# A three-layer graph attention kernel: partial sums stored in the last quarter of a round, loads reordered behind them, two copies moved to ScalarE, one PSUM bank exchanged

## The chip, the cores and the metric

The kernel runs on one core of one Trainium2 chip. The metric is the device time of one execution in microseconds: the median of the runs of one kernel. Differences are judged between kernels run on the same chip.

## The reference

There are 6250 nodes with 64 features each and 206250 directed edges (each of 100000 drawn pairs in both directions, and one loop per node), sorted by destination. Each edge has 64 features of its own, the same in all three layers. A layer is a transformer convolution:

```
q, k, v = x@Wq+bq, x@Wk+bk, x@Wv+bv          # per node
e       = edge_attr @ We                      # per edge
alpha   = sum(q[dst] * (k[src] + e)) / 8      # per edge
w       = softmax of alpha over the edges of one destination
x       = relu(segment_sum((v[src] + e) * w, dst) + x@Ws + bs)
x       = layer_norm(x) * gamma + beta        # after layers 0 and 1 only
```

After the third layer a log-softmax over the features is taken, the input is added, and a last layer norm without scale gives the output.

## The kernel before

**Tiling.** Edges are cut into tiles of 128, six tiles make a chunk (768 edges), four chunks make a unit (`LB = 4`, `TC = 6`). There are 67 whole units and a last one of four tiles. Since edges are sorted by destination, all destinations of a chunk lie within 32 nodes (`W = 32`), so the four chunks of a unit are stacked on 4 x 32 partitions. The weights are folded into the node side, so that an edge's score is a dot product of a 128-vector of its destination (`q`) with the source's 64 features and the edge's own 64 features.

**What is kept in DRAM.** `eaS` holds edge features transposed (feature by edge), `eaP` holds them with edges on partitions, `maskS` a mask that removes the wrong destinations, `keyS` the keys of which the picks (below) are made, `qq` the destination vectors, and `part0` and `part1` one partial sum of 32 rows by 130 columns for each chunk (weighted features, the running maximum, the weight total). The chunks alternate between `part0` and `part1`.

**Two sources of a node's features.** Some of a unit's tiles are gathered by GpSimd, one indirect DMA for each tile (`gather`, L601). The others are *picked*: TensorE multiplies one-hot matrices `hot` (made on VectorE from `keys`, L1335) with the nodes' features that lie in SBUF as `parts` (L1387), and VectorE copies the right block out of PSUM (L1356, L1359). A round picks 12 or 14 of 24 tiles in layers 1 and 2.

**Layer 0 also sorts.** While the first layer runs, `sorter` moves the edges of each unit so that the picked tiles have their sources in known ranges of nodes. A `Move` has four parts of three steps. `row` makes one-hot rows `hit` (L1074), `products` multiplies raw edge features with them (L1085) and, for the destination codes, the `stamp` (L1094). `impress` (L1059) fills `stamp` from `misc` with two VectorE copies (L1064 and L1065) in a move's fourth part for the next move. `index` (L1157) decodes the result: it takes two PSUM tiles from bank "a", `pi` (matmuls L1167) and `pk` (matmuls L1165); VectorE reads `pi` (L1175, L1184), ScalarE reads `pk` (L1186). `Move.across` (L1123) transposes the moved edge features through bank "a" (L1128) and writes `eaP`, `drain` writes `eaS`, `Move.shade` writes `maskS`. Bank "a" has two buffers, bank "g" one.

**A round.** The order of instructions on each engine is the order in which the program writes them; nothing is reordered later, and the SP queue, which issues nearly all loads and stores, works off its list in that order, too. In round `u` of a layer (the loop at L1904) the pieces are these:

- start: the weighted sums of unit `u-2` (`Unit.sums`, L1746, into bank "g", copied by ScalarE to `part`, L1753), and the first half of the scores of unit `u-1` (`Unit.scores`, L1692, which reads `featT` of all four chunks)
- in quarter `j` (0 to 3) of the round: transposes of chunk `j` of unit `u` (`turn`, L1679, copied to `featT` by ScalarE, L1682), a gate that lets GpSimd gather a later chunk (L633), and a quarter of the picks of unit `u+1`
- `turn(j)` begins with `more`, which asks for the edge features of chunk `j+1` of the same unit (`featT <- eaS`, L1659). So `featT` of chunks 1, 2 and 3 is asked for in quarters 0, 1 and 2
- quarter 0 also asks for `eaP` of unit `u+2` (`refill`, L570), runs one step of whatever layer ending is due (`close_up`: `finish` loads the partial sums of up to 512 nodes, L1486, and makes their new features), asks for the four `q` of unit `u+1` (L1633) and, by `Unit.across`, for `featT` of chunk 0 of unit `u+1`
- quarter 1 stores the four partial sums of unit `u-2` (`Line.store`, `Unit.store`, L1757) and appends the `finish` of those nodes that are complete; its first step is taken by the next `close_up`, in quarter 0 of the next round
- quarter 2 asks for the mask of unit `u+1` (`Unit.shade`, L1607) and the keys of unit `u+2` (`decode`, L1831)

`featT` has six buffers. A unit is "placed" when it has gone through the sorter: all whole units in layers 1 and 2, and from unit 3 on in layer 0. Only in layer 0 does SP also load `raw` edge features for the sorter (L1033, eight loads in a move, asked for four parts ahead).

Of the kernel before, what the change touches and what calls it, by code (L numbers as in the profile page):

```python
# [29 lines left out]
BITS = 5  # L30
FAR = 2.0**100
GS = 4
LB = 4
TC = 6
# [395 lines left out]
def main_path(  # L430
# [53 lines left out]
    nc = tc.nc  # L484
# [44 lines left out]
    def ps(tag):  # L529
        return psum.tile([P, 512], F32, tag=tag, name=f"ps_{tag}", bufs={"a": 2, "x": 2}.get(tag, 1))  # L530
# [7 lines left out]
    def placed(layer, k):  # L538

        return k < NT and (layer > 0 or k >= U0)  # L540

    def picked(layer, k):

        if not placed(layer, k) or k < LEAD[layer]:
            return 0
        return 2 if layer == 0 and k <= len(groups) // 2 else PICKS[layer][k % len(PICKS[layer])]
# [501 lines left out]
    class Move:  # L1048
# [10 lines left out]
        def impress(self):  # L1059

            misc, self.pos = marks[self.c0 // GC]
            self.at = (self.c0 % GC) * TC
            spots = slice(self.at, self.at + LB * TC)
            nc.vector.tensor_copy(self.stamp[:, :, :BITS], misc[:, :BITS, spots].rearrange("p r c -> p c r"))  # L1064
            nc.vector.tensor_copy(  # L1065
                self.stamp[:, :, ROW_P : ROW_K + 1], misc[:, BITS:, spots].rearrange("p r c -> p c r")
            )

# [88 lines left out]
        def index(self):  # L1157

            k = self.k
            n = NP  # L1160
            pi = ps("a")[:, : TC * 3 * LB].rearrange("p (t v c) -> p t v c", t=TC, v=3)
            pk = ps("a")[:LB, : n * P].rearrange("c (t h e) -> c t h e", t=n, h=2)
            those = self.to[:, : n * P].rearrange("p (t h e) -> p t h e", t=n, h=2)
            for h in range(2):
                nc.tensor.matmul(pk[:, :, h], keyc[:, h], those[:, :, h], start=True, stop=True)  # L1165
            for t in range(TC):
                nc.tensor.matmul(  # L1167
                    pi[:, t].rearrange("p v c -> p (v c)"),
                    self.to[:, t * P : (t + 1) * P],
                    pickc.rearrange("p v c -> p (v c)"),  # L1170
                    start=True,
                    stop=True,
                )
            mine = src_b[:, k * LB * TC : (k + 1) * LB * TC]
            nc.vector.tensor_tensor(  # L1175
                mine.rearrange("p (c j t) -> p t c j", j=2, t=TC),
                pi[:, :, 0].rearrange("p t (c j) -> p t c j", j=2),
                shift.unsqueeze(2).to_broadcast([P, TC, LB // 2, 2]),
                ALU.add,
            )  # L1180
            nc.vector.tensor_scalar(mine, mine, N - 1, None, ALU.min)
            for h in range(2):
                there = slice(h * P // 2, (h + 1) * P // 2)
                nc.vector.tensor_copy(kbs[there, k], pi[there, :n, 1 + h])  # L1184
            key = small.tile([LB, n, P], FP16, name="key", bufs=1)
            nc.scalar.copy(key.rearrange("c t e -> c (t e)"), pk.rearrange("c t h e -> c (t h e)"))  # L1186
            nc.scalar.dma_start(keyS[k].rearrange("t c e -> c t e"), key)
            moved.add(k)
# [400 lines left out]
    class Unit:  # L1589
# [31 lines left out]
        def ask(self):  # L1621

            self.b = []
            for j in range(self.m):
                b = nc.values_load(
                    base[0:1, self.c + j : self.c + j + 1],
                    engines=(ENG.SP,),
                    min_val=0,
                    max_val=NB * P,
                    skip_runtime_bounds_check_because="the least of a chunk's nodes, NB*128 at most",  # L1630
                )
                self.b.append(b)
                nc.sync.dma_start(self.q[:, j * W : (j + 1) * W], qq[:, ds(b, W)])  # L1633
# [152 lines left out]
    chunks = {}  # L1786
# [30 lines left out]
    def move(n):  # L1817

        for _ in range(n):
            next(sorting, None)  # L1820
            serve()
# [3 lines left out]
    def decode(layer, k):  # L1825

        n = picked(layer, k) if k < NT else 0
        if n and (layer, k) not in keys and (layer or k in moved):
            room = max(PICKS[layer]) * P
            keys[layer, k] = stock[0].tile([P, room], FP16, name="keys")  # L1830
            nc.sync.dma_start(  # L1831
                keys[layer, k][:, : n * P],
                keyS[k].rearrange("t c e -> (t c e)")[: n * P].partition_broadcast(P),
            )
# [43 lines left out]
    def step(n=1):  # L1878
        for _ in range(n):
            advance()  # L1880
# [3 lines left out]
    def close_up(n=1):  # L1884
        step(n)
        for _ in range(n):
            advance(ending)
        if lacking or held:
            reload(current[0] + 1)
# [5 lines left out]
    for layer in range(L):  # L1895
        line = Line(layer)
        assert not picked(layer, 0)

        def free(u, j):
            lead = 2 * LB if not layer else min(2 * LB, LB + u)  # L1900
            release(layer, u * LB + j + (0 if not layer else 1) + lead, nc.scalar.copy)

        picker = Picker(layer)
        for u in range(NU - 2):  # L1904
            this = chunks[layer, u]
            picking = picker.batch(u + 1)
            n = picked(layer, u + 1)
            n //= 2
            pace = 0 if layer else 6 if u < 3 else 3
            while not opened:  # L1910
                move(1)
            line.sums(u - 2)
            line.products(u - 1, 0)
            if waiting:
                active.append(waiting.pop(0))
            for j in range(LB):
                picker.quarter = j
                if j == 2:
                    line.weights(u - 1, 0)
                this.turn(j)  # L1920
                if j == 0:
                    line.refill(u - 2)
                free(u, j)
                if j == 0 and layer:
                    line.most(u - 1, 0)
                    line.products(u - 1, 1, "m")
                if j == 1:
                    line.store()
                    if not layer and placed(0, u + 1):
                        line.most(u - 1, 1)  # L1930
                a, b = -(-n * j // LB), -(-n * (j + 1) // LB)
                if layer:
                    for i in range(max(b - a, 1)):
                        next(picking, None)
                        if not i and not j:
                            line.most(u - 1, 1)
                if j == 0:
                    close_up()
                else:
                    step()  # L1940
                if not layer:
                    move(pace - pace // 2)
                    if j == 0:
                        line.most(u - 1, 0)
                    for _ in range(b - a):
                        next(picking, None)
                    move(pace // 2)
                    picker.evacuate()
                if j == 0:
                    if not layer:  # L1950
                        line.products(u - 1, 1)
                        if not placed(0, u + 1):
                            line.most(u - 1, 1)
                    ask(layer, u + 1)
                    chunks[layer, u + 1].across()
                if j == 2:
                    line.weights(u - 1, 1)
                    chunks[layer, u + 1].shade()
                    decode(layer, u + 2)
            assert next(picking, None) is None  # L1960
            if any(not pair for _, pair, *_ in picker.swaps):
                picker.flush()
            picker.ready.update(keys)
            picker.aim()
            for k in range(u + 2, u + 4):
                decode(layer, k)
# [14 lines left out]
        u = NU - 2  # L1981
# [74 lines left out]
def kernel(tc: tile.TileContext, *args):  # L2056
    nc = tc.nc
    with tc.tile_pool(name="flag", bufs=1) as pool:
        irregular = pool.tile([1, 1], I32, name="irregular")
        with tc.manual_schedule(engines={ENG.PE, ENG.DVE, ENG.Activation, ENG.SP, ENG.Pool}):  # L2060
            main_path(tc, *args, irregular)
        flag = nc.values_load(irregular[0:1, 0:1], min_val=0, max_val=1, skip_runtime_bounds_check_because="a comparison")
        with tc.If(flag > 0):
            general_path(tc, *args)
# [34 lines left out]
```

## Time and profile before

| | |
|---|---|
| runs of the kernel before | 4369.96, 4365.49 and 4349.52 us, median 4365.49 us |
| the profiled execution | 4357.57 us, of which the span is 4355.8 us |
| mean granted TensorE clock | 0.926 |
| DMA | 728.90 MB, mean 167 GB/s |
| the nodes' features of layers 1 and 2 are split into `parts` (L1269) | from 1958.6 us, the last at 3175.9 us |

The span divides into layer 0 with the sorter (up to about 2.0 ms), layer 1 (to about 3.15 ms) and layer 2. In the tables of the profile a row of instructions has its line, engine, operation, what it writes and reads, its count, the busy time and the mean of one in ns, and the idle time of its engine just before it with what ended that idle time. A row of waits has the waiting engine and line, the releaser, the microseconds in total, how many times, and the longest one; "issue" stands for a wait that the profile can put down to nothing. SPq is the list of SP. A window's row has its stretch, then busy us and counts of PE, PEld (weight loads), DVE (VectorE), ACT (ScalarE) and POOL (GpSimd), the granted TensorE clock, the DMA share and GB/s.

### The profile page before, as it was taken

Reading aid. Unit: us, or ns where it says so; the run is one execution under the profiler, and the core shown is the slowest. Engines: PE = TensorE matmul, PEld = TensorE weight load, DVE = VectorE, ACT = ScalarE, POOL = GpSimd, SP = SyncE. Lnnn points to the kernel's source line nnn. Section 1 sums busy time; section 2 is a strip of 40 time slices with the busy share of each in tenths; the row PEclk is TensorE's granted clock in tenths of the full one; section 3 lists DMA queues with packets and bytes.
Section 4 is the critical chain, followed back from the end, with each engine's and each line's share of the span. In section 5 each row is a group of like instructions: output and inputs, shape, how many; then the busy total and the mean of one; then the engine's idle time right before and its main releaser. Section 6 shows DMA issues by size and latency. Waiting matters only on the chain.

```text
span 4355.8 us, 108102 instructions
## 1 busy us (share of the span) xinstructions
PE 3555.1 (82%) x34711; PEld 2476.2 (57%) x34711; DVE 3376.9 (78%) x11892; ACT 2305.6 (53%) x5860; POOL 2706.5 (62%) x2642
## 2 busy tenths in 40 slices
PE   4788888888889898985888888788768878777886
PEld 2345555555555555554666666666556666666664
DVE  6678888888888888865787778787667777777775
ACT  1345555555555555553555555555545556555555
POOL 5467665656666665654776666666367666666662
PEclk9889999999999999997999999999879999999997
DMA  5656666656666666665776667766657666666663
GB/s 124 170 167 189 173 179 166 177 155 181 177 165 185 168 173 158 180 174 136 178 188 167 169 172 180 180 167 172 160 133 182 172 170 172 174 161 169 173 171 88
DMA packets 783500, 728.90 MB, mean 167 GB/s; under 512 B 485192, under 2 KB 610050, under 8 KB 782928
## 3 DMA queue, kind: packets, MB, share of 16 engines
q1 hardware_dynamic: 630436, 508.46, 45.5%
q0 software_dynamic: 84224, 86.41, 10.4%
q10 hardware_dynamic: 68268, 127.03, 8.2%
q8 instruction: 283, 4.64, 0.5%
q14 instruction: 289, 2.37, 0.2%
HBM read 562.78 MB, written 158.68 MB: 166 GB/s over the span
## 4 chain that ended last, share of the span: by engine, by line


## 5 line engine op out<-in xcount | busy, mean ns | idle before, releaser
L601 POOL DMA_INDIRECT feat<-x,gate x1460 | 1451.2, 994 | 706.4 <-issue 315.6
L601 POOL DMA_INDIRECT feat<-in_x,gate x1100 | 1181.8, 1074 | 724.0 <-ACT gate L633 421.0
L1387 PE MATMUL ps_x<-parts,hot 128*128 128x256 f32 x6864 | 1033.1, 299 | 173.5 <-DVE feat L1359 157.3
L1387 PEld LDWEIGHTS ps_x<-parts,hot 128*128 128x128 f32 x6864 | 905.8, 199 | 326.7 <-issue 231.2
L1682 ACT COPY featT<-ps_a 64x384 f32<-64x384 f32 x1588 | 753.7, 475 | 538.0 <-PE ps_a L1679 521.9
L1359 DVE COPY_PREDICATED feat<-which,ps_x 128x128 f32<-128x128 int32 x2574 | 779.0, 303 | 88.7
L1335 DVE TENSOR_SCALAR hot<-keys,rank 128x512 fp32r<-128x512 f16 (+1 forms) x1172 | 471.5, 470 | 59.8 <-DMA keys<-keyS 59.2
L1356 DVE COPY feat<-ps_x 128x128 f32<-128x128 f32 x858 | 246.2, 287 | 301.4 <-PE ps_x L1387 295.6
L1679 PE MATMUL ps_a<-ident,feat 128*128 128x128 f32 x2380 | 433.9, 291 | 53.5 <-DMA feat<-x,src_b 31.2
L1692 PE MATMUL ps_s<-featT,q 128*32 128x384 f32 x2134 | 306.3, 505 | 191.2 <-issue 104.6
L1074 DVE TENSOR_SCALAR hit<-ruler,pos 128x384 bf16<-128x384 f16 x1608 | 457.4, 325 | 5.9 <-PE ps_m L1094 5.9
L1679 PEld LDWEIGHTS ps_a<-ident,feat 128*128 128x128 f32 x2380 | 285.1, 147 | 251.6 <-issue 190.2
L1720 ACT ACTIVATE prob<-prob,part 128x768 f32<-128x768 f32 x204 | 190.3, 933 | 251.1 <-DVE part L1719 155.8
L1746 PE MATMUL ps_g<-feat,probT 128*32 128x128 f32 x9672 | 315.3, 276 | 2.0 <-ACT probT L1737 2.0
L1085 PE MATMUL ps_x<-hit,raw 128*64 128x384 bf16 x1608 | 298.7, 367 | 0.1
L1085 PE MATMUL ps_x<-hit,rest 128*64 128x384 bf16 x1608 | 281.1, 346 | 0.0
L1085 PE MATMUL ps_x<-hit,end 128*64 128x384 bf16 x1608 | 280.5, 345 | 0.0
L1746 PEld LDWEIGHTS ps_g<-feat,probT 128*32 128x32 f32 x9672 | 262.9, 111 | 27.8 <-ACT probT L1737 5.7
L1737 ACT COPY probT<-ps_p 128x384 f32<-128x384 f32 x399 | 191.8, 481 | 124.7 <-PE ps_p L1734 78.9
L1734 PE MATMUL ps_p<-ident,prob 128*128 128x128 f32 x1197 | 212.3, 288 | 37.1 <-ACT prob L1720 33.8
L1692 PEld LDWEIGHTS ps_s<-featT,q 128*32 128x32 f32 x2134 | 71.2, 111 | 267.2 <-issue 194.2
L1706 DVE CUSTOM_DVE_ANT_0 prob<-ps_s,shade 128x384 f32<-128x384 f32 x204 | 112.9, 553 | 129.6 <-PE ps_s L1692 120.3
(266 smaller groups left out, 5288.5 us busy)
## 6 DMA issues: line engine op xcount, KB each, us to landing
featT<-eaS SPq DMA_DIRECT2D x792, 192.0 KB
feat<-eaP SPq DMA_DIRECT2D x134, 768.0 KB
raw<-in_ea SPq DMA_DIRECT2D x536, 96.0 KB
eaS<-eT ACTq DMA_DIRECT2D x134, 384.0 KB
eaP<-feat ACTq DMA_DIRECT2D x128, 384.0 KB
shade<-maskS SPq DMA_DIRECT2D x198, 192.0 KB
keys<-keyS SPq DMA_DIRECT2D x66, 448.0 KB
keys<-keyS SPq DMA_DIRECT2D x66, 384.0 KB
```

Source lines behind the costliest of these rows:

```text
L601: nc.gpsimd.indirect_dma_start(out=feat[:, c, t, 0], out_offset=None, in_=xts[layer][:, :], in_offset=bass.IndirectOffsetOnAxis(ap=index[: ...
L1074: nc.vector.tensor_scalar(hit, ruler, self.pos[:, at : at + 1], None, ALU.is_equal)
L1085: nc.tensor.matmul(self.px[j * D : (j + 1) * D, :HE], self.parts[2 * h + i].thirds[part][:, j, t * D : (t + 1) * D], self.hits[h, 2 * i + ...
L1335: nc.vector.tensor_scalar(hot[:, h], keys[self.layer, k][:, first : first + n], rank[:, h : h + 1], None, ALU.is_equal)
L1356: nc.vector.tensor_copy(found, px[:, :, 0])
L1359: nc.vector.copy_predicated(found, which[:, first : first + 2, b].bitcast(I32).unsqueeze(2).to_broadcast([P, 2, D]), px[:, :, b],)
L1387: nc.tensor.matmul(px[:, v].rearrange("p b d -> p (b d)"), hot[:, h, (2 * pair + v) * P : (2 * pair + v + 1) * P], those[:, i, b0 + h * KB ...
L1679: nc.tensor.transpose(pt[:, t * P : (t + 1) * P], rows[:, 2 * t * D : 2 * (t + 1) * D], ident)
L1682: nc.scalar.copy(featT[:, :, h, :], pt[h * D : (h + 1) * D, : n * P].rearrange("d (i e) -> d i e", e=P))
L1692: nc.tensor.matmul(p_s[rows, :w], self.q[:, rows], self.featT[j][:, cols], start=True, stop=True)
L1734: nc.tensor.transpose(p_t[:, t, :n], self.prob[:n, at : at + P], ident[:n, :n])
L1746: nc.tensor.matmul(p_g[rows, :].rearrange("n (h d) -> n h d", h=2), self.probT[:, t, rows], batch[:, j, t], start=(t == 0), stop=(t == sel ...
```

## The change

Five edits, all in the order or the place of existing work; nothing that is computed changes.

1. The two copies that fill `stamp` run on ScalarE instead of VectorE.
2. `pi` in `index` takes bank "g" instead of bank "a".
3. `line.store()` moves from quarter 1 (after `turn(1)`) to the end of quarter 3.
4. For placed units `chunks[layer, u + 1].across()`, the load of `featT` of the next unit's chunk 0, moves from quarter 0 to quarter 2.
5. In quarter 2 the keys are asked for first, then that `featT`, then the mask; before, it was the mask, then the keys.

```diff
-            nc.vector.tensor_copy(self.stamp[:, :, :BITS], misc[:, :BITS, spots].rearrange("p r c -> p c r"))
-            nc.vector.tensor_copy(
+            nc.scalar.copy(self.stamp[:, :, :BITS], misc[:, :BITS, spots].rearrange("p r c -> p c r"))
+            nc.scalar.copy(
                 self.stamp[:, :, ROW_P : ROW_K + 1], misc[:, BITS:, spots].rearrange("p r c -> p c r")
             )
...
-            pi = ps("a")[:, : TC * 3 * LB].rearrange("p (t v c) -> p t v c", t=TC, v=3)
+            pi = ps("g")[:, : TC * 3 * LB].rearrange("p (t v c) -> p t v c", t=TC, v=3)
...
                 if j == 1:
-                    line.store()
                     if not layer and placed(0, u + 1):
                         line.most(u - 1, 1)
...
                     ask(layer, u + 1)
-                    chunks[layer, u + 1].across()
+                    if not placed(layer, u + 1):
+                        chunks[layer, u + 1].across()
                 if j == 2:
                     line.weights(u - 1, 1)
-                    chunks[layer, u + 1].shade()
                     decode(layer, u + 2)
+                    if placed(layer, u + 1):
+                        chunks[layer, u + 1].across()
+                        chunks[layer, u + 1].shade()
+                if j == 3:
+                    line.store()
```

## The prediction

> **What bounds the kernel now.** I read first the page's table of engines, then busy time by stage, then the waits of TensorE, then the SP queue beside TensorE over two rounds, since the change is mostly to SP's list.
>
> ```profile
> PE 3555.1 (82%) x34711; PEld 2476.2 (57%) x34711; DVE 3376.9 (78%) x11892; ACT 2305.6 (53%) x5860; POOL 2706.5 (62%) x2642
> ```
>
> ```profile
> 300.00:1850.00 1550.00, 1380.77 (x13799) 834.64 (x13795) 1339.57 (x4747) 853.73 (x2175) 983.65 (x914) 0.95 0.66 174
> 2100.00:3050.00 950.00, 786.54 (x7858) 621.17 (x7859) 734.83 (x2536) 523.81 (x1367) 635.51 (x638) 0.95 0.69 175
> 3300.00:4250.00 950.00, 763.87 (x7655) 602.25 (x7654) 730.44 (x2554) 541.31 (x1378) 626.35 (x629) 0.95 0.68 172
> ```
>
> The first stretch lies in layer 0, the others in layers 1 and 2. In layer 0 PE is busy for 89% (1380.77 of 1550) and DVE for 86%: the two take turns waiting for each other. In layers 1 and 2 PE has 82% and DVE 77%, so nobody is full and a wait must be looked for.
>
> ```profile
> PE ps_s L1692 <- issue: 104.6, 41, 4.6
> PE ps_s L1692 <- DMA featT<-eaS: 63.6, 31, 3.9
> ```
>
> ```profile
> DVE prob L1706 <- PE ps_s L1692: 49.6, 19, 5.4
> ```
>
> ```profile
> DVE prob L1706 <- PE ps_s L1692: 56.9, 20, 6.2
> ```
>
> The first two rows are of the whole run, the DVE rows of the windows 2100:3050 and 3300:4250. PE stands before the scores for 168.2 us in 72 waits, 2.3 us each; neither row is among the waits of 300:1850, so this is a thing of layers 1 and 2. The list of SP, then PE, around one such wait:
>
> ```profile
> 2765.92 4.97 SPq L1757 DMA_DIRECT2D part<-part  x4
> 2771.00 0.45 SPq L1659 DMA_DIRECT2D featT<-eaS  x1
> ...
> 2772.64 0.45 SPq L1659 DMA_DIRECT2D featT<-eaS  x1
> 2773.40 0.32 SPq L570 DMA_DIRECT2D feat<-eaP  x1
> 2774.23 2.80 SPq L1633 DMA_DIRECT2D q<-qq  x4
> 2778.24 1.10 SPq L1659 DMA_DIRECT2D featT<-eaS  x2
> 2779.61 6.36 SPq L1757 DMA_DIRECT2D part<-part  x4
> 2786.07 0.47 SPq L1659 DMA_DIRECT2D featT<-eaS  x1
> ```
>
> ```profile
> 2768.11 1.52 PE L1746 MATMUL ps_g<-feat,probT 128*32 128x128 f32 x48
> 2769.45 0.82 PE L1692 MATMUL ps_s<-featT,q 128*32 128x384 f32 x6
> 2774.59 1.32 PE L1692 MATMUL ps_s<-featT,q 128*32 128x384 f32 x2 [4.32 <-issue]
> ...
> 2791.47 1.52 PE L1746 MATMUL ps_g<-feat,probT 128*32 128x128 f32 x48
> ```
>
> A round starts at 2768.11 with the sums. Six of eight score matmuls run (chunks 0 to 2), the two of chunk 3 wait 4.32 us. Their `featT` was issued only at 2771.00, behind four stores that held SP for 4.97 us; from issue to use are 3.6 us. So the "issue" row is the same wait as the featT row: the last edge features of a unit are asked for too late, because the stores stand ahead of them. Why the stores are slow, and how full SP is:
>
> ```profile
> SPq L1757 <- DMA part<-part: 397.8, 208, 4.8
> SPq L1659 <- PE ps_s L1692: 325.5, 49, 14.0
> SPq L570 <- PE ps_g L1746: 188.8, 68, 9.4
> SPq L1757 <- DMA feat<-eaP: 123.6, 61, 3.8
> SPq L1633 <- DMA qq<-qs: 65.8, 16, 8.7
> ```
>
> ```profile
> SPq L570 <- PE ps_g L1746: 85.4, 30, 7.3
> ```
>
> ```profile
> L1607 SPq DMA_DIRECT2D shade<-maskS x57: 356/522/1400, 2108.0 to 3042.5; - x57
> ```
>
> The last two are of 2100:3050. A store waits until the one two places before it, into the same table, has landed (1.9 us a time). With one mask a round, 950 us hold 57 rounds of 16.7 us, of which SP waits for PE (L570) only 1.5: SP is occupied, its DMA waits included, for 15.2 us.
>
> **The change part by part: layers 1 and 2.** With the stores at the end and chunk 0 of the next unit later, chunk 3's `featT` follows `eaP`, four `q` and chunk 2. In the round above it would take the place of the second `featT` of the pair at 2778.24, about 5.4 us after `eaP`, instead of 12.7 (2786.07 - 2773.40): 7 us sooner, against waits of at most 4.6. What moves back has room: chunk 0, mask and stores of this round are read first in the next round's end or later, since unit `u+1` is scored at the start of round `u+2`. The stores stand ahead of the next round's `eaP` and `q`, of units that are summed and scored rounds later. A `finish` loads the table right behind the stores, in quarter 0 as before, and may wait up to 4.8 us for a landing; its data is used a round later, so I cost it at nothing, and at 16 late `q` (8.7 us at most, the qq row) the 7 us still cover the wait that is left.
>
> What is late next? While PE stands, DVE first makes `hot` and then idles: 106.5 us in the two windows of 57 rounds each (49.6 + 56.9), so 123 us for the 132 rounds of two layers. Where both stand the time is surely lost; the other 45 us of 168.2 may only turn into PE waiting for DVE. I take 120 us. Bounds: 168 if all comes back; below, nothing, if SP is simply too full (a rival).
>
> **Layer 0: keys.**
>
> ```profile
> DVE hot L1335 <- DMA keys<-keyS: 59.2, 28, 4.2
> ```
>
> In 28 rounds DVE stands 2.1 us for keys. They now go ahead of the mask, of chunk 0 and of the stores, some 5 us of SP's list (4.97 for the stores alone), but also behind `raw` loads that wait for PE's progress; an advance of 2.1 us on average is enough. Gain up to 59.2 us of DVE; I take it all, the waits being at most 4.2.
>
> **Stamps.**
>
> ```profile
> L1065 DVE COPY stamp<-misc 128x72 bf16<-128x72 bf16 x67 | 20.6, 308 | 0.0
> L1064 DVE COPY stamp<-misc 128x120 bf16<-128x120 bf16 x67 | 18.0, 268 | 0.0
> ```
>
> ```profile
> 1003.89 0.26 DVE L1064 COPY stamp<-misc 128x120 bf16<-128x120 bf16 x1
> ...
> 1004.17 0.55 DVE L1074 TENSOR_SCALAR hit<-ruler,pos 128x384 bf16<-128x384 f16 x2
> ```
>
> By their busy time DVE gets rid of 38.6 us, but they overlap their neighbours: from the first's start to the next instruction's are 0.28 us, times 67 makes 19. I take 20, the row in place. ScalarE takes them up:
>
> ```profile
> L992 ACT CAST misc<-spare x17: 246/266/273, 66.8 to 1818.7; 128x96 bf16<-128x96 int32 x16, 128x72 bf16<-128x72 int32 x1
> ```
>
> ```profile
> ACT to L1115 <- PE ps_m L1094: 181.3, 130, 5.3
> ```
>
> A like copy of 96 columns takes 266 ns there, so two take about 0.53 us, 36 us in all. They stand in the queue ahead of the copies that wait for PE's stamp matmuls (1.4 us a time), which covers them; without that cover PE would wait for ScalarE 0.53 us in 67 moves, the 36 us. The stamp's own reader is a part later. The Trainium skill, "ScalarE: Activation LUTs", section "Rules for kernel authors", speaks against this edit: simple operations belong on VectorE, which it has up to about 3 times faster in bf16. The DVE rows above show no such speed on these strided copies; by the rule the pair would be 1.7 us on ScalarE, 0.3 over the cover, and the sum 23 us worse, an estimate from that page.
>
> **The bank of `pi`.**
>
> ```profile
> PE ps_a L1167 <- ACT key L1186: 19.5, 14, 3.9
> PE ps_a L1128 <- DVE kbs L1184: 18.2, 11, 3.4
> PE ps_a L1167 <- ACT featT L1682: 14.8, 17, 2.3
> PE ps_a L1167 <- DVE xT L1434: 8.0, 4, 2.2
> ```
>
> In 300:1850 PE waits 60.5 us because `pi` needs one of two buffers of bank "a", or holds one. In "g" it follows the sums of the same round, copied out long before, and in some rounds a layer ending's product. Worth 0 to 60 us of PE.
>
> DVE's side is then 59 + 20 = 79 us, PE's 60. Since each spends much of its idle time waiting for the other, the sum of both can't be had; I take their mean, 70 us. Bounds: 30 (half the smaller) to 139 (both). SP's 325.5 us (L1659) stay: with six buffers, chunk 2's `featT` now meets the wait that chunk 0's met, for the same matmuls.
>
> **Sum.** 120 + 70 = 190 us off the profiled 4357.57 gives 4168; that execution lies 8 us under the median of the runs, 4365.49, and against this the forecast is 4175 us. Its own range, from the bounds with 60 to 168 for layers 1 and 2, is 4060 to 4275.
>
> **The rivals.**
>
> *Another wait takes over in layers 1 and 2.* PE's stall is also when DVE makes `hot` for the next picks:
>
> ```profile
> 2769.56 3.05 DVE L1335 TENSOR_SCALAR hot<-keys,rank 128x512 fp32r<-128x512 f16 x8
> ```
>
> That is 3.05 us of work beside 4.32 of stall, 71%. If this share of the 120 us comes back as PE waiting for DVE's `hot` and block copies, 35 are left, and with layer 0's 70 it is 4260 us. For it: PE and DVE are both near 80%. Against it: sums, scores and transposes follow on PE in the same time and cover `hot`.
>
> *The keys come no sooner*, because SP in layer 0 is held at chunk 2 (the 325.5 row) and at `raw`: the change doesn't do there what it says. Layer 0 then gives (20 + 60) / 2 = 40: 4205 us.
>
> *More than the stalls*: without them the clock rises too.
>
> ```profile
> 2180.00:2289.00 109.00, 92.36 (x979) 74.25 (x978) 92.38 (x319) 66.15 (x172) 83.73 (x83) 1.00 0.73 186
> ```
>
> Here the granted clock is 1.00 against 0.95 in the windows. If layers 1 and 2 got there, PE would save 0.05 x 1900 = 95 us; half of it, as DVE must follow, makes 4125 us. Against it: layer 0 has 0.95 without these stalls. The Trainium skill, "TensorE: Matmul & The Clock Gate", section "Part 1: The HAM clock gate", has the clock halved only after about 3.4 us of idleness; by that rule most stalls, 2.3 us on average, cost no clock, and the sum stays at 4175.
>
> *Slower: SP becomes the bound.* SP has 15.2 of 16.7 us. The second store stands eight places behind `eaP` and is what waits for its landing (61 times); chunk 0's `featT` would take that place and that wait. The stores then queue behind keys and two more loads; if each round's wait for their landing goes from 1.9 us to the longest that the row has, 4.8, a round of SP takes 15.2 + 2.9 = 18.1: 1.4 x 132 = 185 us lost, less layer 0's 70, gives 4480 us. It decides once SP's round grows by over 1.5 us. Against it: what queues behind those landings is then needed late.
>
> *Nothing*: the hold behind `eaP` eats the 120 and layer 0's engines find other waits; 4365 us.
>
> **How the numbers follow.** Forecast 0.42, other wait 0.19, keys no sooner 0.12, clock 0.15, slower 0.07, nothing 0.05. A difference under 0.5%, 22 us, is about what a measurement here can't tell from none. All but the last two lie beyond it: faster 0.88, same 0.05, slower 0.07. For the range I take the forecast's own cases and reach down to 4080, short of the clock case's deepest end, and up to 4290, past the 4260 case.
>
> **What would show it.** Right: the featT and "issue" rows of L1692 fall from 168 to under 50 us; the time from `eaP` to chunk 3's `featT` is about 6 us; hot's wait for keys falls under 10; L1167's waits on bank "a" vanish; SP still waits for landings at L1757, now without anyone behind. Wrong: L1692's waits stay, or L570's wait of SP for PE goes to zero (SP is the bound), or PE's wait for L1359 grows by as much as L1692's fell.

## The result, and the profile after

The changed kernel takes 4206.77 us (median of 4 runs, 4198.62 to 4217.09) beside 4367.73 us of the kernel before (4 runs, 4349.52 to 4375.85): the ratio is 0.9638, 95% interval 0.96 to 0.9676. The profiled execution took 4209.98 us, 4208.1 of it span, against 4357.57 and 4355.8 before.

First the page's table of engines, then busy time by stage (per stretch: length, then PE, PEld, DVE, ACT, POOL, the granted clock, the DMA share, GB/s).

```profile
PE 3518.7 (84%) x34711; PEld 2454.2 (58%) x34711; DVE 3349.8 (80%) x11758; ACT 2337.8 (56%) x5994; POOL 2687.5 (64%) x2642
```

```profile
300.00:1750.00 1450.00, 1314.85 (x13206) 790.98 (x13208) 1264.27 (x4437) 844.23 (x2192) 934.24 (x877) 0.95 0.69 179
2060.00:2960.00 900.00, 767.53 (x7723) 606.38 (x7723) 721.05 (x2494) 514.23 (x1343) 623.27 (x629) 0.96 0.75 181
3200.00:4100.00 900.00, 757.28 (x7742) 600.91 (x7742) 738.25 (x2581) 545.49 (x1391) 635.55 (x640) 0.98 0.78 182
```

PE's share rose from 82% to 84%, in layers 1 and 2 from 83% and 80% to 85% and 84% (767.53 and 757.28 of 900). The same matmuls are done in less time.

Where the time came from is read off the weighted sums of the timeline, which fall into three groups with two long pauses, one group for each layer:

| | before, us | after, us | difference |
|---|---|---|---|
| layer 0, to its last sums | 1971.6 | 1930.9 | -40.7 |
| pause between layers 0 and 1 | 77.7 | 77.3 | -0.4 |
| layer 1 | 1096.4 | 1060.7 | -35.7 |
| pause between layers 1 and 2 | 77.9 | 75.0 | -2.9 |
| layer 2 and the end | 1132.2 | 1064.2 | -68.0 |

Two thirds lie in layers 1 and 2. The waits of PE over the whole run (engine, line, what it waited for: us, times, longest):

```profile
PE ps_x L1387 <- DVE feat L1359: 156.7, 185, 2.6
PE ps_s L1692 <- DMA featT<-eaS: 66.4, 40, 4.7
```

The same view cut to 2060:2960 and to 3200:4100, a fence each:

```profile
PE ps_s L1692 <- DMA featT<-eaS: 36.9, 16, 4.7
...
PE ps_s L1692 <- issue: 1.7, 3, 0.9
```

```profile
PE ps_s L1692 <- DMA featT<-eaS: 23.1, 19, 3.4
```

The "issue" row of L1692, 104.6 us before, is 4.5 now; with the featT row, 168.2 us became 70.9. PE's wait for DVE's picks (L1359) was 157.3 us in the same view of before and is 156.7: PE doesn't wait longer for DVE instead. The fall in waits even gives the two layers' own sizes. In layer 1 PE waited 69.2 us of 950 at L1692 before and 38.6 of 900 after, which over 1096 and 1061 us is 80 less 46, 34 us; in layer 2, 75.6 of 950 and 23.1 of 900, which over 1132 and 1064 us is 90 less 27, 63 us. The table has 36 and 68.

The SP queue's own waits, whole run, and then those of 2060:2960:

```profile
SPq L1757 <- DMA part<-part: 533.0, 206, 5.7
...
SPq L1607 <- DMA feat<-eaP: 126.3, 71, 3.9
...
SPq L570 <- PE ps_g L1746: 33.3, 13, 7.5
```

```profile
SPq L570 <- PE ps_g L1746: 6.7, 4, 3.3
```

Two things changed places. The wait behind `eaP` (123.6 us at the second store before) is now the mask's at L1607. And SP hardly waits for PE's sums any more: L570 fell from 188.8 to 33.3 us, in the first window from 85.4 to 6.7, while a store's wait for landing grew from 1.9 to 2.6 us (533.0 / 206). SP still does all that it did, in a shorter round.

SP's list through two rounds of the changed kernel, and the sums and scores of PE beside it:

```profile
2650.06 2.03 SPq L1486 DMA_DIRECT2D both<-part  x2
...
2657.19 3.00 SPq L1659 DMA_DIRECT2D featT<-eaS  x3
...
2681.76 0.35 SPq L570 DMA_DIRECT2D feat<-eaP  x1
2682.62 2.82 SPq L1633 DMA_DIRECT2D q<-qq  x4
2685.55 1.74 SPq L1659 DMA_DIRECT2D featT<-eaS  x3
...
2689.11 5.42 SPq L1757 DMA_DIRECT2D part<-part  x4
```

```profile
2657.77 0.81 PE L1692 MATMUL ps_s<-featT,q 128*32 128x384 f32 x4
2660.67 0.83 PE L1692 MATMUL ps_s<-featT,q 128*32 128x384 f32 x2 [2.08 <-DMA featT<-eaS]
...
2692.15 0.83 PE L1692 MATMUL ps_s<-featT,q 128*32 128x384 f32 x8
```

The second round is the plain case: the features of chunks 2 and 3 of this unit and of chunk 0 of the next go out at 2685.55, the stores come last, and at 2692.15 all eight score matmuls run without a stall. The first round has the loads of a layer ending's tables (L1486 is one of them) ahead of the `q` loads; the features go out only at 2657.19, half a microsecond before PE's scores, and PE waits again. Four score matmuls (chunks 0 and 1) run, and the stall of 2.08 us stands before those of chunk 2.

Two score matmuls belong to each chunk, so the timeline tells round by round whose features PE waits for. Stalls over 0.3 us in 128 rounds of layers 1 and 2:

| PE stalls before the scores of | before | after |
|---|---|---|
| chunk 2 | 9 rounds, 10.5 us | 29 rounds, 59.1 us |
| chunk 3 | 56 rounds, 149.3 us | 14 rounds, 9.5 us |

In each of the 56 rounds of before, chunk 3's scores began 3.1 to 4.6 us (median 3.5) after its features had been asked for: the wait is for these features. It is nearly gone, though a stall for chunk 2 can hide one for chunk 3. Most of what is left is a wait for chunk 2's features, and that one has grown: they go out 11.5 us after the start of the round's sums now, on average, and 9.3 before (2060:2960 and 2100:3050). The 24 rounds whose list has the tables of a layer ending lost 28 of 58 us of these stalls, the other 104 lost 63 of 102.

In layer 0, the waits of DVE in 300:1850, before and then after:

```profile
DVE feat L1356 <- PE ps_s L1387: 29.5, 46, 1.6
...
DVE xT L1434 <- PE ps_a L1432: 2.2, 3, 1.2
```

```profile
DVE feat L1356 <- PE ps_s L1387: 48.0, 65, 2.0
...
DVE xT L1434 <- PE ps_a L1432: 20.0, 13, 4.8
...
DVE hot L1335 <- DMA keys<-keyS: 4.1, 2, 2.2
```

and those of PE after:

```profile
PE ps_s L1692 <- DVE most L1706: 25.3, 30, 2.9
...
PE ps_a L1432 <- DMA xr<-in_x: 14.4, 4, 5.0
...
PE ps_g L1167 <- DVE y L1540: 7.7, 10, 1.5
```

The keys are there in time (53.6 us in this window before, 4.1 after), and L1167 no longer waits on bank "a" (7.7 us in bank "g" are left). But DVE now stands 18.5 us longer for the picks of bank "s" and 17.8 longer at `xT`, and PE waits 14.4 us for loads of `x` (`xr`, L680, the rows from which layer 0's `q` of up to 512 nodes are made) and 11 more for DVE at L1692 (14.2 before). The wait for `xr` and most of that at `xT` are one thing: four stalls of PE between 306 and 454 us, behind which 13.4 of DVE's 20.0 us stand. At the first of them SP's list has

```profile
300.60 4.66 SPq L1757 DMA_DIRECT2D part<-part  x4
...
306.45 0.58 SPq L680 DMA_DIRECT2D xr<-in_x  x1
```

and PE waits 4.99 us, until 311.3. The stores at the end of a round now stand close ahead of the `xr` that the next round asks for and needs at once. Before, the `xr` at this place of the program went out at 302.08 and the stores of its round behind it, at 310.60.

### The profile page after: what moved, and what is told of

Read it like the earlier page. It is cut to its first block, busy times and chain, and to the rows that moved or that the text cites. A ratio compares the mean times of both kernels' runs of the same rounds, so it can differ in the third digit from the quotient of the medians.

```text
span 4208.1 us, 108516 instructions
## 1 busy us (share of the span) xinstructions
PE 3518.7 (84%) x34711; PEld 2454.2 (58%) x34711; DVE 3349.8 (80%) x11758; ACT 2337.8 (56%) x5994; POOL 2687.5 (64%) x2642
## 4 chain that ended last, share of the span: by engine, by line
## 5 line engine op out<-in xcount | busy, mean ns | idle before, releaser
L601 POOL DMA_INDIRECT feat<-in_x,gate x1100 | 1167.8, 1062 | 697.3 <-ACT gate L633 382.5
L1387 PE MATMUL ps_x<-parts,hot 128*128 128x256 f32 x6864 | 1019.2, 297 | 171.5 <-DVE feat L1359 156.7
L1387 PEld LDWEIGHTS ps_x<-parts,hot 128*128 128x128 f32 x6864 | 892.6, 196 | 309.3 <-issue 215.9
L1359 DVE COPY_PREDICATED feat<-which,ps_x 128x128 f32<-128x128 int32 x2574 | 777.7, 302 | 88.6
L1356 DVE COPY feat<-ps_x 128x128 f32<-128x128 f32 x858 | 245.5, 286 | 256.2 <-PE ps_x L1387 245.2
L1692 PE MATMUL ps_s<-featT,q 128*32 128x384 f32 x2134 | 318.3, 509 | 104.8 <-DMA featT<-eaS 66.4
L1136 ACT COPY feat<-ps_a 128x384 f32<-128x384 f32 x256 | 121.8, 480 | 141.1 <-PE ps_a L1128 105.4
L1118 ACT COPY eT<-ps_x 128x384 f32<-128x384 f32 x268 | 129.2, 482 | 125.4 <-PE ps_x L1085 87.8
```

The source lines that it names most:

```text
L601: nc.gpsimd.indirect_dma_start(out=feat[:, c, t, 0], out_offset=None, in_=xts[layer][:, :], in_offset=bass.IndirectOffsetOnAxis(ap=index[: ...
L1356: nc.vector.tensor_copy(found, px[:, :, 0])
L1359: nc.vector.copy_predicated(found, which[:, first : first + 2, b].bitcast(I32).unsqueeze(2).to_broadcast([P, 2, D]), px[:, :, b],)
L1387: nc.tensor.matmul(px[:, v].rearrange("p b d -> p (b d)"), hot[:, h, (2 * pair + v) * P : (2 * pair + v + 1) * P], those[:, i, b0 + h * KB ...
L1692: nc.tensor.matmul(p_s[rows, :w], self.q[:, rows], self.featT[j][:, cols], start=True, stop=True)
```

## The experiments

All twelve runs were made on chips on which the kernel before takes 5656 to 5727 us, not 4366. That has to be understood first, since it decides what each of them can show. The control is the changed kernel itself, run on the same chip as three others:

> The changed kernel itself, as the control on whatever chip this is. If this chip issues TensorE's small matmuls as quickly as the one of the prediction (before about 4365 us), 0.96 again. If it is like the chip of the first four runs (before about 5727 us, where the four edits by themselves gave 0.995, 0.993, 1.002 and 1.001), their sum: about 0.99.

It took 5621.48 us beside 5655.58, ratio 0.9928 (0.99 to 0.9957): the whole change is worth 0.7% here. Its waits of PE over the whole run, and PE's timeline through one unit's sums:

```profile
PE ps_g L1746 <- issue: 632.9, 1001, 1.8
```

```profile
2568.30 1.39 PE L1746 MATMUL ps_g<-feat,probT 128*32 128x128 f32 x41
2570.65 0.32 PE L1746 MATMUL ps_g<-feat,probT 128*32 128x128 f32 x2 [0.97 <-issue]
...
2573.52 0.29 PE L1746 MATMUL ps_g<-feat,probT 128*32 128x128 f32 x1 [1.02 <-issue]
```

In these lines 41 matmuls go out at the usual pace, and the last ones then trickle, one or two each 0.7 us, though nothing that the profile shows holds them. On the first chip all 48 take 1.52 us and this row doesn't exist. A round of layers 1 and 2 lasts 22.5 us on average instead of 16.1, and SP waits for PE's sums (L570) for 887.0 us of the run. The granted clock was 0.84 to 0.87 in these runs, against 0.93 to 0.94 on the first chip; whether that is a cause of the pauses or follows from them isn't shown.

**One edit at a time.** Each of the four edits by itself, against the kernel before:

```
e1  stores        j == 1: line.store()  ->  j == 3: line.store()
e2  bank          pi = ps("a")  ->  ps("g")
e3  stamps        nc.vector.tensor_copy(self.stamp...)  ->  nc.scalar.copy (both)
e4  order         placed units: decode, across(), shade() all in quarter 2
```

> Only the stores move, to the end of quarter 3; chunk 0's featT stays in quarter 0 and the mask ahead of the keys. Theory A (the stores ahead of chunk 3's features are what made TensorE wait in layers 1 and 2): this alone brings 90 to 125 us of the 161, and the featT and issue waits of L1692 fall from 168 us to 50 to 90. Theory B (the stores and the other loads must both go, since chunk 0's featT is also ahead of chunk 3's): 40 to 70 us, waits of L1692 above 100 us.

Measured 5703.17 beside 5726.73 us, 0.9954 (0.9931 to 0.9976).

> Only pi moves from bank a to bank g. Theory A (layer 0 is paced by VectorE and TensorE in turn, so a wait that goes is half given back): 10 to 25 us. Theory B (TensorE's 60 us of waits at L1167 and L1128 end on VectorE's next result anyway): under 8 us, with the waits moved to other lines of bank a.

Measured 5692.16 us, 0.9933 (0.991 to 0.9957).

> Only the stamps' two copies move to ScalarE. Theory A (VectorE paces layer 0): 10 to 20 us, by the 0.28 us between the two starts times 67. Theory B (VectorE has other waits to fill): within 6 us of no change, and the rule of the Trainium skill, ScalarE: Activation LUTs, section Rules for kernel authors, would make it up to 23 us slower; the copies' own duration on ScalarE tells, 0.25 to 0.30 us each by the like copies against 0.8 to 0.9 by the rule.

Measured 5732.17 us, 1.0017 (0.9997 to 1.0037).

> Chunk 0's featT moves to quarter 2 and the keys stand ahead of it and of the mask; the stores stay in quarter 1. Theory A: the stores still stand ahead of chunk 3's features, so layers 1 and 2 stay within 15 us and the waits of L1692 above 120; layer 0 loses the 59 us of VectorE's waits for keys only in part, and gains 10 to 30 us. Theory B (chunk 0's featT was as much in the way as the stores): 50 us or more, L1692 below 100.

Measured 5730.49 us, 1.0007 (0.9986 to 1.0028).

On this chip the bank and the stores are worth some half a per cent each, by intervals that overlap, and stamps and order can't be told from nothing. The wait that the stores were to remove is hardly there to begin with. The waits of PE in the run with the stamps alone, whose SP list is that of the kernel before:

```profile
PE ps_s L1692 <- issue: 10.7, 16, 2.4
...
PE ps_s L1692 <- DMA featT<-eaS: 8.0, 4, 3.5
```

18.7 us, where the first chip had 168.2. So these four don't say how the first chip's 161 us divide among the edits.

**Stores, then order, then the rest.** On the chip of the control two more were run:

```
f2  = e1 again
f3  = e1 + e4 (stores and order; stamps and bank as before)
```

> Before, with the stores alone moved from quarter 1 to quarter 3. Theory: in layers 1 and 2 the wait of PE for chunk 3's edge features was there because the stores stood ahead of them; this edit alone takes those rows of L1692 from 168 us to about 70 and gives most of what layers 1 and 2 gained (98 us from stage to stage), 0.975 to 0.98 on a chip with before at 4365. Rival: what counts is that chunk 0 and the mask come later (order); then the store alone gives under 30 us, over 0.993, and L1692 stays over 120 us. On a chip with before at 5727, about 0.995 as in the first run of this edit.

Measured 5629.16 beside 5655.58 us, 0.9949 (0.9926 to 0.9973).

> The stores moved and chunk 0, the mask and the keys reordered; stamps and bank as before. Theory: layers 1 and 2 as in the whole change; hot's wait for the keys in layer 0 (59 us) goes to under 10 and layer 0 gets at most half of it, as PE is the next late: 0.968 to 0.975 with before at 4365, so that bank and stamps are worth under 20 us. Rival: layer 0's gain of 36 us is the bank's, so that this kernel shows no gain in layer 0: its last sums stay at about 1965 us. With before at 5727: 0.995.

Measured 5620.64 us, 0.995 (0.9928 to 0.9973). As an end to end time f2, f3 and the whole change (0.9928) can't be told apart. What the stores alone do to SP's list can be read on any chip. One round each of the stamps-alone run (list as before) and of the stores-alone run f2:

```profile
2975.86 0.32 SPq L570 DMA_DIRECT2D feat<-eaP  x1
...
2981.50 1.10 SPq L1659 DMA_DIRECT2D featT<-eaS  x2
2982.85 3.52 SPq L1757 DMA_DIRECT2D part<-part  x4
2986.80 0.12 SPq L1659 DMA_DIRECT2D featT<-eaS  x1
```

```profile
2984.99 0.34 SPq L570 DMA_DIRECT2D feat<-eaP  x1
...
2988.81 1.70 SPq L1659 DMA_DIRECT2D featT<-eaS  x3
```

In the upper list the third `featT` after `eaP`, chunk 3's, goes out behind the four stores, 10.9 us after `eaP`; in the lower one it is the last of three in a row. Over the rounds of a stretch in layer 1, medians from `eaP` to the issue of chunk 3's features:

| run | us after `eaP` | `eaP` after its round's sums, mean | round, mean |
|---|---|---|---|
| before, first chip, 2100:3050 | 12.5 | 2.8 | 16.7 |
| changed, first chip, 2060:2960 | 4.8 | 6.0 | 16.1 |
| stamps alone (list as before), 2750:3950 | 10.1 | 6.9 | 22.6 |
| stores alone (f2), 2750:3950 | 5.7 | 7.2 | 22.3 |
| changed (f1), 2750:3950 | 5.0 | 7.5 | 22.5 |

Of the advance on the second kind of chip, 5.1 us, the stores bring 4.4 and the order 0.7 (the order by itself, e4, has 9.1 us, 1.0 less than the list of before). But with rounds of 22.6 us the features were early anyway, 18.1 us into the round by the means (6.9 and 11.1), so that an earlier issue has nothing to remove.

**Stores split.** If SP is the bound now, taking its landing waits away must help:

```
if j == 2:
    ...
    if layer:
        stores of chunks 0 and 1
    chunks[layer, u + 1].across(); shade()
if j == 3:
    stores of chunks 2 and 3   (layer 0: all four)
```

> The changed kernel, with the stores of chunks 0 and 1 in quarter 2, ahead of chunk 0's features and the mask, in layers 1 and 2: the stores of chunks 2 and 3 then find the landings of the first two mostly over. Theory: SP is now the bound of layers 1 and 2 (it waits for PE in only 11 us of two windows of 900 us); the landing wait of 2.5 us a round shrinks to under 1.2 us, and the 66 us that PE still waits for features at L1692 fall to under 30: 30 to 65 us off the changed kernel, 0.95 to 0.957 with before at 4365. Rival: PE and DVE hold each other (L1359's 157 us) and SP only just keeps up: the landing wait shrinks all the same, but the time stays within 15 us of the changed kernel and SP's wait for PE at L570 grows by what was saved. With before at 5727 both say the same as the changed kernel.

Measured 5619.2 us, 0.9933 (0.9906 to 0.9959). SP's waits in the split kernel and then, for the same two things, in the control:

```profile
SPq L570 <- PE ps_g L1746: 1063.4, 109, 17.6
...
SPq L1759 <- DMA part<-part: 100.8, 107, 4.6
```

```profile
SPq L570 <- PE ps_g L1746: 887.0, 113, 15.0
...
SPq L1757 <- DMA part<-part: 175.7, 105, 5.0
```

75 us of landing waits went, 176 us of waiting for PE came, and the time is the control's. With rounds this long that is what both theories say; on the first chip it wasn't tried.

**What makes the sums slow here.** The kernel before with fewer, wider matmuls in the sums; it leaves out the right weights for four of a unit's six tiles:

```
-for t in range(self.tiles):           one tile, 128 columns, 24 calls a unit
+for t in range(0, TC, 3):             three tiles, 384 columns, 8 calls a unit
     matmul(p_w[rows], self.probT[:, t, rows], batch[:, j, t : t + 3], ...)
```

> The kernel before, with a unit's weighted sums in 8 wide matmul calls (three tiles, 384 columns, against one tile's weights) in place of 24 narrow ones: TensorE streams as many columns in a third of the instructions. This leaves out the right weights for four of a unit's six tiles; all other work stays. Theory: in the eight runs so far what sets the time is TensorE's supply of instructions in the sums (some 600 us of waits named issue before L1746, none in the run of the prediction); with a third of the instructions those waits fall under 100 us, the sums take about 1.5 us again, and the time falls from about 5700 to 4300 to 4600 us, as SP's order then counts once more. Rival: the slow sums come from what they read or from the clock; then they stay as slow and the time stays over 5400 us.

Measured 5354.82 beside 5723.38 us, 0.9351 (0.931 to 0.9392). Its waits of PE:

```profile
PE ps_x L1387 <- issue: 127.8, 159, 6.4
PE ps_s L1692 <- issue: 81.5, 53, 7.9
...
PE ps_g L1749 <- issue: 36.8, 46, 2.6
...
PE ps_s L1692 <- DMA featT<-eaS: 30.1, 15, 4.1
```

The sums no longer trickle (some 630 us of issue waits in the narrow form, 36.8 at L1749 now), so the number of narrow matmuls, or of the weight loads that went with them, was what slowed them. The forecast of 4300 to 4600 us failed: the sums' busy time and issue waits together fell from 1357 us (stamps alone, same chip) to some 400, but the time by only 369, and it stays a thousand above the first chip's. PE's waits named issue at all other lines rose from 129 to 415 us; at L1387 they were 56 in the run with the stamps alone and are 127.8 here. So the pauses moved in part to other matmuls, and what makes them stays open.

This run shows one thing more. Its list is that of before, and its rounds are still long, 21.2 us on average; but with short sums the scores start 2.1 us after them on average, not some 7. The wait at L1692 is back, 111.6 us in the two rows where it was 18.7. Some of the issue part can be the pauses; but of the 30 rounds in which chunk 3's scores were due less than 2.5 us after its features had been asked for, 29 stalled, for 86.5 us, and they started at a median of about 3 us after the issue. SP is not full in this run: at L570 alone it waits over 600 us.

**SP loaded.** Is the wait at L1692 a matter of how full SP is? Fourteen loads of 8 KB that nobody reads, at the end of each round of layers 1 and 2:

```
+if layer:
+    for _ in range(14):
+        spare = work.tile([P, W], BF16, name="spare2", bufs=8)
+        nc.sync.dma_start(spare, maskS[0, :, :W])
```

> The kernel before with 14 more small loads on SP's queue at the end of each round of layers 1 and 2, which nobody reads (output unchanged). In the runs so far, on chips where the kernel before takes 5650 to 5730 us, SP waits about 8 of 22.6 us a round for PE's sums, against 1.5 of 16.7 in the run of the prediction; 14 loads of some 0.45 us bring it to about 2. Theory: PE's wait for edge features at L1692 comes with SP's fullness: it rises from under 20 us to over 100, and the time by 1 to 4%. Rival: that wait had another cause (TensorE's speed in the first run): L1692 stays under 40 us and the time within 1% of the kernel before.

Measured 5658.59 beside 5661.8 us, 0.9995 (0.9971 to 1.002). SP's wait for PE's sums in 2750:3950, in the stamps-alone run and then in this one:

```profile
SPq L570 <- PE ps_g L1746: 425.9, 49, 17.2
```

```profile
SPq L570 <- PE ps_g L1746: 35.2, 21, 4.0
```

and PE's waits at L1692 in the loaded run:

```profile
PE ps_s L1692 <- DMA featT<-eaS: 19.7, 13, 3.8
...
PE ps_s L1692 <- issue: 12.0, 20, 3.4
```

The load worked: SP's slack went from 8 us a round to 0.7, less than the 1.5 of the first chip. Yet L1692 has 31.7 us, not over 100, and the time didn't move. My theory as I had written it, that the wait comes with SP's fullness, fell.

> The changed kernel with the same 14 loads a round in layers 1 and 2. Theory: with chunk 3's features ahead of the stores, the wait at L1692 stays under half of that of the kernel before with the loads, and the ratio of the two is 0.97 to 0.985, of which 0.993 is there without loads. Rival: SP is now simply the bound and its order doesn't matter, or it isn't and order doesn't matter either: both kernels with loads stand in the ratio 0.993 as without.

Measured 5627.47 us, 0.9942 (0.9919 to 0.9966): by the medians 0.9945 of the loaded kernel before, as without loads. The rival's line came true.

> Before with the stores alone moved to quarter 3, and the same 14 loads. Theory: the stores ahead of chunk 3's features were the cause, so layers 1 and 2 come out as in the whole change with loads (stage times within 1%), and L1692 too. Rival: the later place of chunk 0 and the mask does it: layers 1 and 2 then stay near the kernel before with loads.

Measured 5651.47 us, 0.9994 (0.9972 to 1.0017). Its profiled execution, 5613.58 us, is the quickest of its twelve, so its stage times prove nothing; by the medians the stores alone gain nothing under load that can be measured. Without load two runs of this edit gave 0.5% each (0.9954 and 0.9949).

What is left is a narrower theory: not how full SP is, but when chunk 3's features go out, against when its scores come. The loads were put behind chunk 3's features in the list; they moved `eaP` from 6.9 to 9.9 us after its sums and chunk 3's issue from 18.1 to 21.2, still ahead of scores that come some 7 us into the next round, behind the slow sums. On the first chip it was 15.5 us (2.8 and 12.7), and from issue to use 3.6 us, 19.1 in all, against scores due at 18.1 (a round of 16.7 and 1.4 us of sums). The run with the wide sums agrees: there the scores come early again, and the wait is back without SP being full.

The rounds agree, too. Of the runs on these chips with narrow sums, looked at in layers 1 and 2 (from 2500 us on), those with the stores in quarter 1 have a few rounds in which PE stalls at chunk 3's scores: 2 and 3 in bank and stamps alone, 3 in order alone, 9 in the loaded kernel before. The seven runs with the stores later (stores alone twice and once loaded, stores and order, the changed kernel, loaded too, and the split one) have none. So on these chips the place of the stores decides whether this wait is there. How much of the first chip's time it is worth by itself no run shows, since none with a single edit was made there.

## Why the prediction came out as it did

The forecast was 4175 us, 190 off; measured are 161 off by the medians (147.6 between the two profiled executions; the rest is that before was profiled 10 us under its median and after 3 over).

- **Layers 1 and 2, 120 us: right.** Measured are 104 by the stage table, 97 by the waits at L1692. The mechanism is the one named: chunk 3's features no longer queue behind the stores, and PE's stalls for them fell from 149.3 to 9.5 us. "5.4 us after `eaP`" is 4.8 in the median.
- **"7 us sooner": half of it.** This step left out that SP's list would slide against PE: `eaP` goes out 6.0 us after its round's sums began, not 2.8. Chunk 3's features go out at 12.2 us (6.0 and 6.2, means), not 15.5, so 3.3 us sooner. The list got no shorter while the round did, by 0.6 us, and landings grew by 0.7 us each. For chunk 3 the 3.3 us were enough in most rounds. But the slide makes chunk 2's features late, which the prediction didn't look at: their stalls grew from 10.5 to 59.1 us, and that is why 70.9 us stay at L1692, above the "under 50" that was set as the sign.
- **"A `finish` loads the table ... I cost it at nothing": right for layers 1 and 2 in that nothing got worse**, as the rounds with an ending lost 28 of their 58 us; but they are the slowest to gain, 24 of 128 rounds with 30 of the 69 us that are left. In layer 0 "what moves back has room" missed a load: the stores now stand ahead of `xr`, which is needed at once, and PE waits 14.4 us for it.
- **Layer 0, 70 us: mis-sized, 40.7 measured.** The removed waits were right: keys 53.6 to 4.1, L1167's on bank "a" gone. The term that was mis-sized is the mean of both engines' sums, which has no place for new waits. DVE got back 49.5 us at the keys and lost 36 at L1356 and `xT`; PE lost 25 at L1432 and L1692. The lower bound of 30, half of the smaller engine's, was nearer than the mean. How the 40.7 divide among keys, bank and stamps no run shows.
- **Stamps, 20 us:** nothing by themselves (1.0017), on the other chips. The two copies take more on ScalarE than the 0.53 us that I took:

```profile
L1064 ACT COPY stamp<-misc x67: 395/405/420, 71.6 to 1838.6; 128x120 bf16<-128x120 bf16 x67
L1065 ACT COPY stamp<-misc x67: 333/343/363, 71.9 to 1838.9; 128x72 bf16<-128x72 bf16 x67
```

  405 and 343 ns, against 268 and 308 on VectorE. The rule of the Trainium skill, "ScalarE: Activation LUTs", section "Rules for kernel authors", points the right way, but its factor of up to 3 is 1.3 here for the pair (1.5 and 1.1); and the cover held, for no wait of PE for these copies appears.
- **The bank, up to 60 us:** on the other chips it is 0.7% by itself (0.4 to 0.9); on the first chip it can't be parted from the rest of layer 0.
- **The eighth place behind `eaP`: misread.** It is the mask (126.3 us), not chunk 0's features, and in layers 1 and 2 the keys still go out behind the stores, asked for at the end of the round. The mask isn't needed until the next round, so this cost nothing that shows.
- **The rivals.** Another wait takes over: not that for DVE, as L1359 stayed (157.3, 156.7); what grew is the wait for chunk 2's features. Keys no sooner: its 4205 us is within 2 us of the measured time, but the keys row rules it out; a time that fits isn't evidence for its story. The clock: 0.95 to 0.96 and 0.98, some of what was asked for; PE's busy time a round fell only from 13.8 to 13.7 us (786.54 / 57, 767.53 / 56). SP the bound: its sign, L570 near zero, came, and yet the kernel got faster. The sign was badly chosen: without slack SP was late with chunk 2's features, but that cost less than chunk 3's gave back. Whether SP now limits layers 1 and 2 on the first chip stays open.

## What to carry to other kernels

When loads and stores share a queue, ask for each entry how long after the start of the round it goes out and when its reader comes, not only how full the queue is: a load behind slow stores costs something only if its reader comes before it has landed. When an item is moved forward on a nearly full queue, expect the queue itself to slide; here that took half of the advance. Then ask the same question of every other entry: here the next chunk's features, and the loads that follow the stores at their new place, became the late ones. And where two engines take turns waiting for each other, a mean of what each gets back is no forecast until the waits that may be new are in it; here the smaller side's half came nearer.

## What the runs showed of the hardware

The same program took 4366 us where the prediction was made and 5656 to 5727 us on the chips of the experiments, each steady within 0.6% of its median. On the latter, streams of narrow matmuls run dry: about 1000 waits of up to 2.0 us, some 630 us in all, stand before the weighted sums with no semaphore to blame. A third of the matmul instructions for the same columns ended them there and brought 6.5% back, while waits of the same name grew at other lines. The Trainium skill, "Runtime: NRT & Kernel Launch", section "Instruction fetch mechanics", has the fetch of instructions run ahead and hidden behind their issue; on the first chip nothing speaks against that, and whether fetch is what falls short on the others no run here shows. A change that is worth 3.6% on one chip can be worth 0.7% on another of the same kind, where TensorE's pauses in the sums make the round longer.
